# Two broadcast rows joined into one 4 KB-per-partition transfer, and a new due time for the added-up tiles

## The chip, the cores and the metric

The kernel runs on one core of one Trainium2 chip. The metric is the device time of one execution in microseconds (us), as the median of several runs. On the core, TensorE (PE), VectorE (DVE), ScalarE (ACT) and GpSimd (POOL) each follow their own instruction list in order; SyncE (SP) issues most of the DMAs, and POOL issues those that add one tile to another.

## The reference

Four graph layers are applied to `x` of shape (64, 256, 128): 64 graphs of 256 nodes with 128 features, all with one 256x256 matrix `adj`. Each layer is `x = x + layer(relu(layernorm(x)))`. Layer 0 is a gated recurrent unit of five steps, layer 1 a Chebyshev convolution, layer 2 a normalised convolution, layer 3 attention with an additive score. Nearly all the work lies in the score of layer 3:

```python
pre = s1[:, :, None, :] + s2[:, None, :, :] + b_lin      # (4 dims: graph, i, j, e)
h = jnp.where(pre >= 0, pre, ALPHA * pre)
e = jnp.einsum('bije,e->bij', h, a) + bias               # 256 features e
attn = jax.nn.softmax(e, axis=2)
out = jax.nn.sigmoid(jnp.einsum('bij,bjf->bif', attn, x))
```

For every graph and every pair of nodes (i, j) a piecewise linear function of 256 features is summed.

## The kernel before

**Units of work.** Two graphs form a pair, so there are 32 pairs (`NPAIR`). For each pair, `front(p)` computes layers 0 to 2 and the projections that the scores need. The scores themselves are cut into 64 slots a pair (`SLOTS`), and a slot covers four nodes i. For each slot two tiles `rl` of 128 x 2048 f32 (1 MB) are made, one from each half of the 256 features. DVE makes one tile of the first half in one instruction (L853), ACT makes one tile of the second half in eight (L867), and POOL makes tiles of either half in eight (L875). PE sums a tile over the features with four matmuls into a bank of 128 x 512 (L935, in `score`). `tail(p, ic)` turns a finished block of 32 slots into attention and output; there are two blocks a pair.

**Joined slots.** In 3 of 10 slots (`SHARE`, `WITH`) the two tiles are not both given to PE. `add_pair` (L890) lets a DMA, issued by POOL, add tile `z` onto tile `t` (L892), and PE then scores `t` once. There are 13 `rl` tiles in all, so `z` is wanted again for the next slots.

**The planner.** The order of the instructions on each engine is worked out when the program is built. A loop keeps a clock for each engine (`ran`) and for the SP queue (`moved`), and gives the next step to the engine whose clock stands lowest. Nothing of these clocks is left in the program but the order. A tile carries the planned time from which it may be used: `tile_ready` compares it, and `work_on_tile` takes the free tile with the earliest one. For an added-up tile, `add_pair` plans this time from `ISSUE`, `ADDED` and `LANDED` (L28): in `adding` the additions stand in a row of 5.2 us each, and 2.4 us are put on top. Both the freed `z` and the summed `t` get this time. If a planned time is too early, the engine that takes the tile stands still in the program until the DMA has landed, with all that stands behind it on that engine.

**The two rows.** The odd one of the 256 features is not scored on the tiles. Its contribution needs, for a pair, two rows of 512 numbers on all 128 partitions: `s2o` and `lin`. `front` makes both as a piece `quarter` of 128 partitions x 128 numbers, in which the numbers of the two rows stand on partitions 0, 32, 64, 96 and 1, 33, 65, 97. `quarter` is written to a DRAM tile `row` (L698). Two DMAs then read from it, `s2o` and `lin`, each with four pieces of 512 B a partition that stand 16 KB apart in `row` (L701); the source is the same for all partitions. `tail` uses `s2o` on DVE (L738) and `lin` on POOL (L748).

Of the kernel before, what the change touches and what calls it, by code (L numbers as in the profile page):

```python
# [8 lines left out]
F32 = mybir.dt.float32  # L9
# [5 lines left out]
P = 128  # L15
NB = 2
# [8 lines left out]
SHARE = (3, 10)  # L25
AHEAD_OF = 2
LOW = 1
ISSUE, ADDED, LANDED, SLACK = 0.65, 5.2, 2.4, 0.3  # L28


@with_exitstack
def kernel(
# [50 lines left out]
    nc = tc.nc  # L83
    B, N, D = x.shape
# [6 lines left out]
    work = ctx.enter_context(tc.tile_pool(name="work", bufs=2))  # L91
    relu_pool = ctx.enter_context(tc.tile_pool(name="relu", bufs=3))
    psum = ctx.enter_context(tc.tile_pool(name="psum", bufs=1, space=PSUM))
    dram = ctx.enter_context(tc.tile_pool(name="dram", bufs=4, space=bass.MemoryType.DRAM))
# [11 lines left out]
    def ran(engine, us, *after):  # L106
        start = max(clock[engine], 0.0, *after)
        if engine == ACT:
            behind[0] = max(0.0, behind[0] - (start - clock[ACT])) + 0.024 * us
        clock[engine] = start + us  # L110
        return clock[engine] + SEEN[engine] + (behind[0] if engine == ACT else 0.0)

    def moved(since):

        queue[0] = max(queue[0], since) + 0.5
        return queue[0] + 2.2
# [3 lines left out]
    def take():  # L120

        spare.sort(key=lambda b: b[1])
        return spare.pop(0)
# [7 lines left out]
    last, done = {}, [0]  # L131
# [268 lines left out]
    def flat(t):  # L400
        return t.rearrange("p b n -> p (b n)")
# [34 lines left out]
    def feat(name, **kw):  # L436
        return work.tile([P, NB, N], F32, name=name, **kw)
# [13 lines left out]
    def norm(src, since, h):  # L451

        stats = work.tile([P, NB * NC, 3], F32, name="stats")
        mv = work.tile([P, NB * NC, 2], F32, name="mv")
        s, h = rows_of(src), rows_of(h)[:, :, 0:D]
        yield DVE, since
        for k in range(0, NB * NC, 2):
            nc.vector.bn_stats(stats[:, k:k + 2, :].rearrange("p k s -> p (k s)"), s[:, k:k + 2, :].rearrange("p k d -> p d k"))
        t = ran(DVE, 0.8, since)
        yield POOL, t  # L460
        inverse_root(mv[:, :, 1], stats[:, :, 2], 1.0 / D, OP.mult, LN_EPS, OP.add)
        t = ran(POOL, 1.45, t)
        yield DVE, t
        nc.vector.scalar_tensor_tensor(mv[:, :, 0], stats[:, :, 1], -1.0, mv[:, :, 1], op0=OP.mult, op1=OP.mult)  # L464
        t = ran(DVE, 0.1, t)
        yield ACT, t
        for k in range(NB * NC):
            nc.scalar.activation(h[:, k, :], s[:, k, :], AF.Relu, bias=mv[:, k, 0:1], scale=mv[:, k, 1:2])  # L468
        return ran(ACT, 1.55, t)

    def copied(name, bank, t):

        c = feat(name, **(SHORT if name not in KEPT else KEPT[name]))
        nc.scalar.copy(c, by_feature(bank[0]))  # L474
        t = ran(ACT, COPY, t)
        spare.append([bank[0], t])
        return c, t
# [5 lines left out]
    def front(p):  # L483
# [8 lines left out]
        t = yield from norm(x0, 20.0 if p else 3.0, h)  # L492
        yield PE, t, 1
        b = take()
        to_feature(b[0], h)
        t_h = t
        t = ran(PE, TURN, t, b[1])
        yield ACT, t
        hT, t_hT = copied("hT", b, t)
        for step in range(STEPS):  # L500
            yield PE, t_h, 1, lambda: "adj" in SET_UP
            b = take()
            mix_nodes(b[0], h, adj_t)
            t = ran(PE, MIX, t_h, b[1])
            yield ACT, t
            mT, t_m = copied("mT", b, t)
            if p == 0:
# [6 lines left out]
                t = ran(PE, PROJECT, t_m)  # L514
# [3 lines left out]
            else:  # L518
# [4 lines left out]
                t = ran(PE, 2 * PROJECT, t_m, t_hT, pr[1])  # L523
# [3 lines left out]
            t = ran(ACT, TANH, t, r[1])  # L527
# [4 lines left out]
            if p == 0:  # L532
# [5 lines left out]
                t = ran(PE, PROJECT, t_rh)  # L538
            else:
# [7 lines left out]
                t = ran(PE, 2 * PROJECT, t_rh, pv[1])  # L547
# [6 lines left out]
            if p < 1:  # L554
                nc.scalar.activation(pv[0], pv[0], AF.Tanh, bias=bh, scale=1.0)
                t = ran(ACT, TANH, t)
                yield DVE, t
                nc.vector.tensor_sub(d, by_feature(pv[0]), hT)
                t = ran(DVE, ELEMENTS, t)
            else:  # L560
                nc.scalar.activation(d, by_feature(pv[0]), AF.Tanh, bias=bh, scale=1.0)  # L561
                t = ran(ACT, TANH, t)
# [3 lines left out]
                t = ran(POOL, 1.3, t)  # L566
            yield DVE, max(t, t_z)
            nc.vector.scalar_tensor_tensor(by_feature(pr[0]), by_feature(pr[0]), 1.0, d, op0=OP.add, op1=OP.mult)  # L568
            t = ran(DVE, ELEMENTS, t, t_z)
# [8 lines left out]
            b = take()  # L578
            to_token(b[0], hT)
            t = ran(PE, TURN, t_hT, b[1])  # L580
# [9 lines left out]
        t = ran(DVE, ELEMENTS, t)  # L590
# [6 lines left out]
        b = take()  # L597
        mix_nodes(b[0], h, adj_n)
        t = ran(PE, MIX, t_h, b[1])
# [3 lines left out]
        b = take()  # L603
        to_feature(b[0], h)
        t = ran(PE, TURN, t_h, b[1])
        yield ACT, t
        hT, t = copied("hT", b, t)
        yield PE, t_h, 1
        b = take()
        mix_nodes(b[0], h, adj_2)  # L610
        t = ran(PE, MIX, t_h, b[1])
        yield ACT, t
        c2T, t = copied("c2T", b, t)
# [3 lines left out]
        t = ran(PE, PRODUCTS, t, po[1])  # L617
# [3 lines left out]
        t = ran(DVE, ELEMENTS, t)  # L621
# [3 lines left out]
        t = ran(DVE, ELEMENTS)  # L625
# [4 lines left out]
        t = yield from norm(x2, t, h)  # L630
        yield PE, t, 1
        b = take()
        mix_nodes(b[0], h, adj_ti)
        t = ran(PE, MIX, t, b[1])
        yield ACT, t
        yT, t = copied("yT", b, t)
# [3 lines left out]
        t = ran(PE, PRODUCT, t, po[1])  # L640
# [3 lines left out]
        t = ran(DVE, ELEMENTS, t)  # L644
# [3 lines left out]
        t = ran(ACT, COPY, t)  # L648
# [3 lines left out]
        t = ran(DVE, ELEMENTS, t)  # L652
        yield POOL, t
        inverse_root(rn, rn, MOST_POSITIVE, OP.min, NORM_EPS * NORM_EPS, OP.max)
        t = ran(POOL, 1.35, t)
# [6 lines left out]
        t = ran(DVE, 1.04, t)  # L662
# [5 lines left out]
        t = yield from norm(x3, t, h3)  # L668
        yield PE, t, 1
        b = take()  # L670
        to_feature(b[0], h3)
        t = ran(PE, TURN, t, b[1])
# [11 lines left out]
        b = take()  # L684
# [4 lines left out]
        t = ran(PE, 0.6, t_hT, b[1])  # L689
        yield ACT, t  # L690
        quarter = work.tile([P, P], F32, name="quarter", bufs=1)
# [2 lines left out]
        nc.scalar.activation(s1o, b[0][:, P:P + NB * NC], AF.Identity, bias=b_odd, scale=1.0)  # L694
        t = ran(ACT, 0.35, t)
        spare.append([b[0], t])
        row = dram.tile([P, P], F32, name="row", bufs=2)
        nc.sync.dma_start(row, quarter)  # L698
        lin, s2o = feat("lin"), feat("s2o")
        for k, o in enumerate((s2o, lin)):  # L700
            nc.sync.dma_start(flat(o).rearrange("p (q n) -> p q n", q=4), row[1 - k:P:32, :].unsqueeze(0).to_broadcast([P, 4, P]))  # L701
            t = moved(t)
        t = moved(t)
        t_lin = t
        yield PE, t_hT, 1
        b = take()
        project(b[0], w2n[:, P:2 * P], hT)
        t = ran(PE, PROJECT, t_hT, b[1])
# [3 lines left out]
        b = take()  # L712
        project(b[0], w1[:, P:2 * P], hT)
        t = ran(PE, PROJECT, t_hT, b[1])
# [6 lines left out]
        b = take()  # L721
        project(b[0], w1[:, 0:P], hT)
        t = ran(PE, PROJECT, t_hT, b[1])
# [6 lines left out]
                        lin=lin, t_lin=t_lin, since=(max(t_n, t_s2a), max(t_b, t_2), max(t_b, t_2)))  # L730
# [77 lines left out]
    adding = [0.0]  # L808
# [81 lines left out]
    def add_pair(n):  # L890
        (since, t, e), (since_z, z, e_z) = pairs[n][0], pairs.pop(n)[2]
        nc.gpsimd.dma_start(out=t.rearrange("p g b n -> p (g b n)"), in_=z.rearrange("p g b n -> p (g b n)"), accum_op=OP.add)  # L892
        issued = ran(POOL, ISSUE, since, since_z)
        adding[0] = max(adding[0], issued) + ADDED
        done = adding[0] + LANDED
        held[e] -= 1
        held[e_z] -= 1
        tiles.append([z, done])
        made.append((done, n, 2, t, None))
# [53 lines left out]
    def begin_front():  # L953
        p = begun_fronts[0]
        if p > 0:
            load_x(p + 1)
        begin(p, front(p))
        begun_fronts[0] += 1
# [27 lines left out]
    while scored[0] < 2 * NSLOT or CHAINS:  # L986
# [20 lines left out]
        if ready:  # L1007
            if e == PE and len(tiles) <= LOW:
                ready = [x for x in ready if x[1] == (2,)] or ready
            _, (rank, *_), what = min(ready, key=lambda x: x[1])  # L1010
            if rank < 2:
                advance(what)
            elif e == PE:
                score(what)
            elif rank == 2:
                add_pair(what)
            else:
                work_on_tile(e)
            in_order()
            now[e] = max(now[e], clock[e])  # L1020
        else:
            later = [x[0] for x in todo] + [t for t in now.values() if t > now[e]]
            now[e] = min(later) if later else now[e] + 1.0
# [31 lines left out]
```

## Time and profile before

| What | Value |
|---|---|
| Median of 3 runs | 5011.35 us (5008.55 to 5022.84) |
| Profiled execution, its own time | 4997.03 us |
| Its span from the first to the last instruction | 4995.2 us |
| TensorE clock granted, mean | 0.993 of full speed |
| Busy: PE, DVE, ACT, POOL | 4851.9, 4659.2, 4664.4, 4662.2 us |
| DMA: adding DMAs (L892) | 614 of 1 MB each |
| DMA: `row`, `s2o`, `lin` | 32 each, of 64, 256 and 256 KB |
| Share of the 16 DMA engines' span taken by the POOL queue | 64.2% |

The busy times are those of the whole execution, with about 130 us at the start in which only the first pair's front runs. A DMA line of the profile gives the count, the size of each transfer, and the median time from its issue to its landing. An idle time is put down to what ended it.

### The profile page before, as it was taken

How to read it: one execution, taken by the hardware profiler on the slowest of the kernel's cores; microseconds unless marked ns; L12 is line 12 of the kernel's file. 1: busy time of each engine (PE TensorE's matmuls, PEld its weight loads, DVE VectorE, ACT ScalarE, POOL GpSimd, SP SyncE). 2: the span in 40 equal slices, each digit the busy share in tenths (PEclk: the TensorE clock that was granted, in tenths of full speed). 3: DMA queues.
4: the chain of work that ended last, by engine and by line, in shares of the span. 5: the costliest groups of instructions: out<-in, count | busy, mean ns of one | idle time of the engine just before them, and what ended most of it. 6: DMA issues, size and time to landing. Idle time of an engine off the chain costs nothing.

```text
span 4995.2 us, 134047 instructions
## 1 busy us (share of the span) xinstructions
PE 4851.9 (97%) x52487; PEld 1789.2 (36%) x52487; DVE 4659.2 (93%) x3289; ACT 4664.4 (93%) x12177; POOL 4662.2 (93%) x9446
## 2 busy tenths in 40 slices
PE   8999999999999999999999999999999999999988
PEld 3333333333333333333333333333333333333332
DVE  3999999999999999999999999999999999999998
ACT  3999999999999999999999999999999999999998
POOL 1999999999999999999999999999999999999997
PEclk9999999999999999999999999999999999999999
DMA  0667766677677676776676677776667766666677
GB/s 18 122 141 145 148 141 137 138 144 145 139 143 144 135 147 136 142 144 141 136 152 129 139 145 144 143 144 140 135 138 145 144 136 139 142 138 140 140 156 147
DMA packets 165644, 689.42 MB, mean 138 GB/s; under 512 B 14864, under 2 KB 86416, under 8 KB 86416
## 3 DMA queue, kind: packets, MB, share of 16 engines
q0 software_dynamic: 88416, 643.86, 64.2%
q1 hardware_dynamic: 75872, 36.98, 3.1%
q8 instruction: 410, 6.72, 0.5%
q14 instruction: 226, 1.85, 0.1%
q10 hardware_dynamic: 720, 0.00, 0.0%
HBM read 26.48 MB, written 10.49 MB: 7 GB/s over the span
## 4 chain that ended last, share of the span: by engine, by line
PE 55%; POOL 13%; DVE 13%; DMA 7%; ACT 7%; issue 4%; POOLq 0%; ACTq 0%; DVEq 0%
PE bank L935 32%; PE bank L398 19%; DVE rl L853 11%; POOL rl L875 10%; DMA rl<-rl 7%; ACT rl L867 5%; PE bank L426 2%; POOL rl L892 1%; PE bank L419 1%; POOL d L565 1%; DVE hT L572 1%; DVE bank L568 1%; PE bank L688 1%; PE bank L686 1%; ACT h L468 0%
## 5 line engine op out<-in xcount | busy, mean ns | idle before, releaser
L853 DVE TENSOR_TENSOR rl<-s1a,bank 128x2048 f32<-128x2048 f32 x1814 | 4060.1, 2277 | 173.7 <-PE bank L935 79.7
L867 ACT ACTIVATE rl<-bank,s1b 128x256 f32<-128x256 f32 x10128 | 4045.9, 757 | 144.8 <-PE bank L935 94.6
L875 POOL TENSOR_SCALAR rl<-s2n,s1b 128x256 f32<-128x256 f32 x6256 | 2949.0, 659 | 113.2 <-DMA rl<-rl 59.9
L935 PE MATMUL bank<-rl,win_n 128*32 128x512 f32 x17728 | 2227.4, 596 | 57.4 <-DVE rl L853 34.7
L935 PE MATMUL bank<-rl,win 128*32 128x512 f32 x10128 | 1335.5, 595 | 0.0
L935 PEld LDWEIGHTS bank<-rl,win_n 128*32 128x32 f32 x17728 | 559.0, 110 | 1235.2 <-issue 991.9
L875 POOL TENSOR_SCALAR rl<-s2c,s1a 128x256 f32<-128x256 f32 x1872 | 895.6, 655 | 14.3 <-DMA rl<-rl 7.0
L892 POOL DMA_DIRECT2D rl<-rl x614 | 567.8, 935 | 38.2 <-DVE rl L853 14.2
L935 PEld LDWEIGHTS bank<-rl,win 128*32 128x32 f32 x10128 | 327.3, 110 | 657.5 <-issue 534.5
L398 PE MATMUL bank<-mT,wts 128*32 128x512 f32 x2560 | 336.6, 592 | 1.3 <-DVE rh L530 1.3
L398 PE MATMUL bank<-adj_t,h 128*32 128x256 f32 x5120 | 308.7, 382 | 4.7 <-ACT h L584 4.7
L565 POOL TENSOR_TENSOR d<-d,hT 128x512 f32<-128x512 f32 x155 | 219.4, 1416 | 66.6 <-ACT d L561 66.6
L398 PEld LDWEIGHTS bank<-adj_t,h 128*32 128x32 f32 x5120 | 164.8, 111 | 179.9 <-issue 62.1
L468 ACT ACTIVATE h<-x,mv 128x128 f32<-128x128 f32 x384 | 187.8, 806 | 6.1 <-DVE mv L464 6.0
L398 PE MATMUL bank<-rh,u5t 128*32 128x512 f32 x1280 | 172.4, 601 | 15.3 <-DVE rh L530 15.3
L398 PE MATMUL bank<-mT,w 128*32 128x512 f32 x1280 | 170.6, 594 | 0.0
L398 PE MATMUL bank<-hT,wts 128*32 128x512 f32 x1280 | 167.8, 593 | 0.0
L561 ACT ACTIVATE d<-bank,gate_b 128x512 f32<-128x512 f32 x155 | 145.3, 937 | 22.6 <-PE bank L398 22.4
L526 ACT ACTIVATE bank<-bank,gate_b 128x512 f32<-128x512 f32 x160 | 138.3, 864 | 20.4 <-PE bank L398 19.5
L398 PEld LDWEIGHTS bank<-mT,wts 128*32 128x32 f32 x2560 | 83.6, 110 | 193.8 <-issue 152.1
L549 ACT ACTIVATE bank<-bank,gate_b 128x512 f32<-128x512 f32 x160 | 146.7, 917 | 6.7 <-PE bank L398 6.7
L474 ACT COPY mT<-bank 128x512 f32<-128x512 f32 x160 | 127.5, 797 | 26.1 <-PE bank L398 25.8
(166 smaller groups left out, 3501.2 us busy)
## 6 DMA issues: line engine op xcount, KB each, us to landing
rl<-rl POOLq DMA_DIRECT2D x614, 1024.0 KB, 8.0
xin<-in_x_dram SPq DMA_DIRECT2D x64, 128.0 KB, 4.7
s2o<-row SPq DMA_DIRECT2D x32, 256.0 KB, 8.6
lin<-row SPq DMA_DIRECT2D x32, 256.0 KB, 11.0
out_dram<-o SPq DMA_DIRECT2D x64, 128.0 KB, 4.6
row<-quarter SPq DMA_DIRECT2D x32, 64.0 KB, 2.9
w_raw<-in_L_gnn_w_w_dram SPq DMA_DIRECT2D x3, 128.0 KB, 2.6
th_raw<-in_L_gnn_Theta_dram SPq DMA_DIRECT2D x1, 320.0 KB, 3.5
```

Of the source, the lines that this page charges most:

```text
L398: nc.tensor.matmul(o[g:g + 32], w[:, g:g + 32], t, start=start, stop=stop, skip_group_check=True)
L468: nc.scalar.activation(h[:, k, :], s[:, k, :], AF.Relu, bias=mv[:, k, 0:1], scale=mv[:, k, 1:2])
L474: nc.scalar.copy(c, by_feature(bank[0]))
L526: nc.scalar.activation(r[0], pr[0], AF.Tanh, bias=br, scale=0.5)
L549: nc.scalar.activation(pr[0], pr[0], AF.Tanh, bias=bz, scale=0.5)
L561: nc.scalar.activation(d, by_feature(pv[0]), AF.Tanh, bias=bh, scale=1.0)
L565: nc.gpsimd.tensor_sub(d, d, hT)
L853: nc.vector.tensor_tensor(t, rows.to_broadcast(whole), ops["s2a"].unsqueeze(1).to_broadcast(whole), op=OP.min)
L867: nc.scalar.activation(t[:, g, b, :], s2p[:, b, :], AF.Relu, bias=ops["s1"][1][:, b, i:i + 1], scale=-1.0)
L875: nc.gpsimd.tensor_scalar(t[:, part, b, :], ops["s2n" if k else "s2c"][:, b, :], ops["s1"][min(k, 1)][:, b, row], MOST_NEGATIVE, op0=OP.mi ...
L892: nc.gpsimd.dma_start(out=t.rearrange("p g b n -> p (g b n)"), in_=z.rearrange("p g b n -> p (g b n)"), accum_op=OP.add)
L935: nc.tensor.matmul(pe[g * 32:(g + 1) * 32, :], w[:, 31 - r:63 - r], flat(t[:, g]), start=False, stop=(left[block] == 0), skip_group_check= ...
```

## The change

The change has two parts. In `front`, the DRAM tile `row` becomes 2 x 512 numbers, each of the two rows contiguous, and one after the other. Two DMAs of four partitions each write it. One DMA then reads the whole 4 KB for each of the 128 partitions into one SBUF tile `rows`, of which `lin` and `s2o` are the two halves. The planned time of arrival (`t_lin`) is changed with it. In `add_pair`, the planned time of a summed tile is worked out in another way: 6.6 us after its issue, or 5.3 us after the addition before it, whichever is later.

```diff
-ISSUE, ADDED, LANDED, SLACK = 0.65, 5.2, 2.4, 0.3
+ISSUE, ADDED, LANDED, SLACK = 0.65, 5.3, 6.6, 0.3
...
-        row = dram.tile([P, P], F32, name="row", bufs=2)
-        nc.sync.dma_start(row, quarter)
-        lin, s2o = feat("lin"), feat("s2o")
-        for k, o in enumerate((s2o, lin)):
-            nc.sync.dma_start(flat(o).rearrange("p (q n) -> p q n", q=4), row[1 - k:P:32, :].unsqueeze(0).to_broadcast([P, 4, P]))
-            t = moved(t)
-        t = moved(t)
+        row = dram.tile([2, NB * N], F32, name="row", bufs=2)
+        for k in range(2):
+            nc.sync.dma_start(row[k].rearrange("(q n) -> q n", q=4), quarter[k:P:32, :])
+            t = moved(t) if k else max(t, moved(t) - 2.2)
+        rows = work.tile([P, 2, NB, N], F32, name="rows")
+        nc.sync.dma_start(rows.rearrange("p k b n -> p (k b n)"), row.rearrange("k t -> (k t)").unsqueeze(0).to_broadcast([P, 2 * NB * N]))
+        lin, s2o = rows[:, 0], rows[:, 1]
+        t = moved(t) + 1.5
         t_lin = t
...
         issued = ran(POOL, ISSUE, since, since_z)
-        adding[0] = max(adding[0], issued) + ADDED
-        done = adding[0] + LANDED
+        done = adding[0] = max(adding[0] + ADDED, issued + LANDED)
```

## The prediction

> **What bounds the kernel now.** I read the busy times first, then the waits, then the DMA issues, then one stretch in time.
>
> ```profile
> PE 4851.9 (97%) x52487; PEld 1789.2 (36%) x52487; DVE 4659.2 (93%) x3289; ACT 4664.4 (93%) x12177; POOL 4662.2 (93%) x9446
> ...
> DVE rl L853 <- PE bank L935: 79.7, 108, 2.9
> DVE rl L853 <- DMA rl<-rl: 76.8, 28, 7.9
> POOL rl L875 <- DMA rl<-rl: 66.9, 18, 7.8
> ACT rl L867 <- DMA rl<-rl: 46.0, 21, 6.2
> PE bank L935 <- DMA rl<-rl: 21.6, 20, 4.9
> ...
> rl<-rl POOLq DMA_DIRECT2D x614, 1024.0 KB, 8.0
> s2o<-row SPq DMA_DIRECT2D x32, 256.0 KB, 8.6
> lin<-row SPq DMA_DIRECT2D x32, 256.0 KB, 11.0
> row<-quarter SPq DMA_DIRECT2D x32, 64.0 KB, 2.9
> ```
>
> All four engines are close to full, so no idle time is free. The waits for the adding DMA (us, times, longest) are few but long: up to 7.9 us. Where they lie shows in the timeline around one broadcast, from answers for SP, POOL and DVE, with the landing times of that stretch and of a quiet one before it, and with three windows (the last two numbers are the DMA share and GB/s):
>
> ```profile
> 2060.70 0.36 SPq L701 DMA_DIRECT2D s2o<-row  x1
> 2061.11 0.50 SPq L701 DMA_DIRECT2D lin<-row  x1
> 2060.86 1.04 POOL L892 DMA_DIRECT2D rl<-rl  x1
> 2077.39 8.88 DVE L853 TENSOR_TENSOR rl<-s1a,bank 128x2048 f32<-128x2048 f32 x4 [6.35 <-DMA rl<-rl]
> 2082.65 3.61 POOL L875 TENSOR_SCALAR rl<-s2n,s1b 128x256 f32<-128x256 f32 x8 [6.87 <-DMA rl<-rl]
> ...
> DMA to landing us min/median/max: 15.8/16.2/16.5
> DMA to landing us min/median/max: 7.3/7.5/7.6
> ...
> 127.50:139.00 11.50, 8.15 (x77) 2.19 (x69) 9.13 (x9) 10.51 (x28) 9.66 (x21) 0.98 0.23 47
> 2062.00:2067.00 5.00, 5.00 (x72) 2.24 (x68) 3.55 (x5) 4.47 (x14) 4.83 (x11) 1.00 0.24 39
> 2072.00:2078.00 6.00, 5.40 (x56) 1.56 (x52) 0.61 (x1) 6.00 (x16) 3.78 (x9) 1.00 1.04 216
> ```
>
> The addition issued at 2060.86 lands after 16.5 us, where 7.5 is usual, and the two behind it are as late. While the broadcasts flow, the DMA engines move 39 GB/s at a share of 0.24; when the addition moves, 216. The first pair's broadcast (127.5 to 139) has no addition beside it and still gets 47 GB/s. So the two broadcasts are slow in themselves (512 KB at 45 GB/s is 11.4 us), and an addition stands behind them with idle DMA engines.
>
> I then laid a window from 10 to 35 us after the s2o issue on each of pairs 1 to 31, and one from 40 to 65 us. Their sums, in this order:
>
> ```profile
> sum 775.00, PE 720.85 PEld 223.09 DVE 656.53 ACT 682.94 POOL 674.77; mean PE 23.25 PEld 7.20 DVE 21.18 ACT 22.03 POOL 21.77
> sum 775.00, PE 757.53 PEld 251.32 DVE 763.24 ACT 768.67 POOL 760.27; mean PE 24.44 PEld 8.11 DVE 24.62 ACT 24.80 POOL 24.52
> ```
>
> After a broadcast, DVE, ACT and POOL lose 107, 86 and 85 us more than in the quiet windows (763.24 - 656.53, and so on), 93 on average; PE loses 37 more. Over 130 to 4960 us the windows view gives PE 4723.88 us busy of 4830, which leaves 106 idle.
>
> **What the Trainium skill says.** "DMA: Bandwidth & Descriptors" has three places. Its section "Issuing engines are not separate DMA queues" says that DMAs of SP and POOL share the same 16 engines and interleave; the trace agrees that they share, at 16.5 against 7.5 us. Its section "Queues, rings and completion order" says that an engine alternates between queues packet by packet; the trace does not look like that, as the addition waits for most of s2o. Its section "Latency and other measured facts" reports copies from HBM rows at large power-of-two pitches running at half rate, and suspects channels that are hit in lockstep. No trace here has such rows, but the 47 GB/s from pieces 16 KB apart, the same for every partition, could be of that kind. The section "Anatomy of one DMA" gives 2.0 us + bytes/436e3: an estimate of 3.2 us for 512 KB. For the 1 MB addition it gives 4.4, where the trace's shortest is 6.7, so I use it as a lower end only.
>
> **The change part by part.**
>
> 1. *Three transfers of a pair.* Before, SP issues `row`, `s2o`, `lin`: 0.34 + 0.36 + 0.95 us. After, two writes and one read, about the same; SP mostly waits for other engines (1743.7 us for `x` alone), so this costs nothing, and out_dram stores behind it have no reader on the chip. The writes use four partitions each, which no row shows: between the shortest `row` landing (1.5 us) and the longest (9.8); I take 3.
> 2. *The broadcast.* Both move 512 KB. Pieces fall from 1024 of 512 B to 128 of 4 KB. If the pace goes by pieces or by the 16 KB pitch, the flow falls from 11.4 us to between 1.2 (512 KB at 436 GB/s) and 3 us (four times the pace of now); if it goes by bytes from one place, it stays at 11.4. I take 3. Nobody waits for `rows` itself: the first L738 after the load at 2060.70 runs at 2126.35, 65 us later.
> 3. *The additions.* Of the 614, 86 overlap a broadcast or queue behind one that does; they land after 12.3 us on average, the others after 8.1 (both from the trace's records). The excess 4.2 falls with the flow, by some 3/4.
> 4. *What this is worth.* If the three elementwise engines alone set the pace, all of 93 us comes back; if PE does, only its 37. Both limits bind in turn: DVE also waits 79.7 us for PE to free tiles, and the 106 us of PE idle include waits that stay (31.9 for hT of L572, 16.5 for rh of L530). For a full cure I take 60, between 37 and 93; three quarters of it is 45.
> 5. *The due times.* A lone addition is planned to land 0.65 + 0.13 + 5.2 + 2.4 = 8.4 us after its start before (0.13 is the planner's POOL constant), 0.65 + 0.13 + 6.6 = 7.4 after. In a row the step is 5.3 instead of 5.2. The trace has 7.3 (median of the lone ones) and 5.3. So the plan becomes right at the median and loses 1 us of margin. In the trace I followed each tile of the 528 additions outside the broadcasts to its next user: the next writer of `z` starts a median 3.0 us after the landing, but 112 start within 1.2 us; for PE on `t` 56 start within 1.5 us. Were every one of these due 1.1 us sooner, the writers would wait 67 us more in all, 22 per engine, and PE 31. The program is also re-sorted: the PE list differs in most places, though the counts hold (1813 L853 instead of 1814, 235 groups of eight L875 `s2c` instead of 234). Tiles free 1 us sooner may give some of it back. I take a loss of 5, between a gain of 15 and a loss of 31. Behind a waiting L853 stand the hT and rh steps on DVE, for which PE waits.
>
> Sum against the profiled execution: 4997 - 45 + 5 = 4957 us. The median of the runs stands 14 above that execution, so the forecast is 4971.
>
> **Rivals.**
>
> *The flow stays slow, and the plan does no harm.* The change then doesn't do what it says for the additions. For it: 47 GB/s with no addition in flight may be the pace of reading one place, whatever the piece. Against it: 16 KB between pieces is a special address step, and the change takes it away. Gain 0, plan -5 to +10: 5005 to 5020.
>
> *Slower: the margin in the due times is missed.* Place: the next writer of `z` (L853, L867, L875) and L935 on `t`. Price: 22 to 31 us as in part 5, and more if late landings stay, since the plan then expects tiles in 7.4 us that come in 12 to 16. It decides from the point at which the stall brings back less than about 10 us. Time: 5011 + 30 = 5041. For it are the 112 writers within 1.2 us; against it the usual slack of 3.0 us for writers and 5.0 for PE.
>
> *The elementwise engines set the pace throughout.* The whole 93 us and a better plan: 5011 - 93 - 5 = 4913. Against it: PE would be left with some 10 us of idle time in 4800.
>
> **How the numbers follow.** A measurement of this kernel can tell about 0.3% (15 us) from no change. I give the forecast's case (a gain of 16 to 75 us) 0.64, the full return 0.04, the slow flow without harm 0.16 and the missed margin 0.16. Faster is 0.68, same 0.16, slower 0.16. The range goes from 4920, near the full return, to 5020, the top of the slow flow; the missed margin is left out.
>
> **What would show it.** Right: `rows<-row` lands within about 5 us, additions next to it within 9 to 10, their longest is well below 18.3, and the waits on `DMA rl<-rl` of DVE, POOL and ACT, 190 us together now, fall below 100. Part 5 is wrong if these waits stay small per wait but grow in number away from the broadcasts. The forecast is wrong if `rows<-row` takes over 10 us, or if PE is as idle as before (106 us) while the long waits are gone.

## The result, and the profile after

The changed kernel takes 4958.24 us (median of 4 runs, 4956.34 to 4965.92) against 5013.7 for the kernel before (median of 4): a ratio of 0.989, with a 95% interval of 0.9872 to 0.9909. The profiled execution of after is 4965.92 us, of before 4997.03. The latter lies 17 us below the median of its kernel, so the two traces show only 31 of the 55 us.

The page of the kernel after, with busy times and DMA issues (no landing is recorded for `rows`, as for other SP transfers of this run):

```profile
PE 4840.3 (98%) x52487; PEld 1793.6 (36%) x52487; DVE 4663.4 (94%) x3288; ACT 4672.1 (94%) x12177; POOL 4684.9 (94%) x9454
...
rl<-rl POOLq DMA_DIRECT2D x614, 1024.0 KB, 7.9
rows<-row SPq DMA_DIRECT2D x32, 512.0 KB
```

The waits of the kernel after for the adding DMA (us in total, times, longest):

```profile
DVE rl L854 <- DMA rl<-rl: 39.1, 32, 3.7
ACT rl L868 <- DMA rl<-rl: 36.6, 24, 3.4
PE bank L935 <- DMA rl<-rl: 25.8, 27, 3.2
POOL rl L876 <- DMA rl<-rl: 16.6, 19, 2.0
```

DVE, ACT and POOL together wait 92 us instead of 190. But the number of their waits has not fallen: 75 now, 67 before. The long ones are gone (3.7 at most, 7.9 before), and short ones have come.

The same pair as before in the timeline of the kernel after, with the landing times of the additions issued from 2055 to 2085 us, and the window in which the broadcast flows:

```profile
2059.22 0.34 SPq L702 DMA_DIRECT2D rows<-row  x1
2061.58 0.75 POOL L893 DMA_DIRECT2D rl<-rl  x1
...
DMA to landing us min/median/max: 7.2/7.4/9.0
...
2060.00:2063.00 3.00, 3.00 (x40) 1.10 (x36) 3.00 (x2) 3.00 (x8) 3.00 (x7) 1.00 0.72 210
```

While the broadcast flows the DMAs move 210 GB/s instead of 39, and no engine but PE's weight loads is idle in that window. By the trace's records the last of the 128 pieces ends a median 5.7 us after the issue (3.2 to 9.4). The additions in flight together with a broadcast land after 8.9 us on average; in the kernel before it was about 12.

The windows from 10 to 35 us after each `rows` issue, and from 40 to 65, for pairs 1 to 31 of the kernel after:

```profile
sum 775.00, PE 770.38 PEld 245.77 DVE 741.52 ACT 742.43 POOL 753.64; mean PE 24.85 PEld 7.93 DVE 23.92 ACT 23.95 POOL 24.31
sum 775.00, PE 758.62 PEld 258.34 DVE 756.42 ACT 768.29 POOL 759.38; mean PE 24.47 PEld 8.33 DVE 24.40 ACT 24.78 POOL 24.50
```

After a broadcast the three elementwise engines now lose 15, 26 and 6 us more than in the quiet windows, where it was 107, 86 and 85. PE loses nothing there.

### The profile page after: what moved, and what is told of

Same layout as the page of the kernel before. It is cut to its first block, busy times and chain, and to the rows that moved or that the text cites. A ratio compares the mean times of both kernels' runs of the same rounds, so it can differ in the third digit from the quotient of the medians.

```text
span 4964.1 us, 133991 instructions
## 1 busy us (share of the span) xinstructions
PE 4840.3 (98%) x52487; PEld 1793.6 (36%) x52487; DVE 4663.4 (94%) x3288; ACT 4672.1 (94%) x12177; POOL 4684.9 (94%) x9454
## 3 DMA queue, kind: packets, MB, share of 16 engines
q14 instruction: 225, 1.84, 0.1%
## 4 chain that ended last, share of the span: by engine, by line
PE 58%; POOL 11%; DVE 8%; DMA 4%; ACT 4%; issue 3%; POOLq 0%; DVEq 0%; ACTq 0%
PE bank L935 36%; PE bank L398 18%; POOL rl L876 8%; DVE rl L854 6%; DMA rl<-rl 4%; ACT rl L868 3%; PE bank L426 2%; POOL rl L893 1%; PE bank L688 1%; PE bank L686 1%; PE bank L419 1%; POOL d L565 1%; DVE mv L464 0%; POOL mv L393 0%; DVE hT L572 0%
## 5 line engine op out<-in xcount | busy, mean ns | idle before, releaser
L935 PE MATMUL bank<-rl,win_n 128*32 128x512 f32 x17728 | 2198.3, 595 | 56.6 <-DVE rl L854 29.7
```

The costliest lines, as they stand in the source:

```text
L935: nc.tensor.matmul(pe[g * 32:(g + 1) * 32, :], w[:, 31 - r:63 - r], flat(t[:, g]), start=False, stop=(left[block] == 0), skip_group_check= ...
```

## The experiments

**The two parts, each alone.** The planned arrival of the rows turned out not to change the order: with one part alone, every instruction of the four engines stands exactly where it stands in the kernel before (rows alone) or after (due times alone). So with these two runs and the changed kernel, each step is a change either of the broadcast or of the order. The changed kernel was run again as the mark.

> The changed kernel once more, as the mark for the other runs of this chip. Every theory expects a ratio of 0.989 to the kernel before, some 4958 us where that has 5013.

Measured: 4969.38 us against 5015.43 of before on this chip; ratio 0.9905 (0.9889 to 0.9922).

The joined rows with the old due times:

```diff
-ISSUE, ADDED, LANDED, SLACK = 0.65, 5.3, 6.6, 0.3
+ISSUE, ADDED, LANDED, SLACK = 0.65, 5.2, 2.4, 0.3
...
-        done = adding[0] = max(adding[0] + ADDED, issued + LANDED)
+        adding[0] = max(adding[0], issued) + ADDED
+        done = adding[0] + LANDED
```

> The joined broadcast alone, with the due times of before; PE, DVE, ACT and POOL have their instructions in exactly the order of before. Theory A (an addition stood behind the slow broadcast, and the new due times cost a little): 10 to 15 us faster than the changed kernel, a ratio of about 0.987 to before, and the waits for the adding DMA away from the broadcasts stay at some 35 us over DVE, ACT and POOL. Theory B (the due times bring the gain): hardly faster than before, a ratio over 0.996.

Measured: 4934.2 us, ratio 0.984 (0.9824 to 0.9856). That is 81 us below before and 35 below the changed kernel, more than theory A expected on both sides. Its waits for the adding DMA:

```profile
ACT rl L868 <- DMA rl<-rl: 20.0, 16, 2.5
POOL rl L876 <- DMA rl<-rl: 13.6, 9, 2.5
DVE rl L854 <- DMA rl<-rl: 9.0, 11, 1.8
PE bank L936 <- DMA rl<-rl: 8.4, 13, 2.3
```

43 us over the three engines, of which 33 lie away from the broadcasts (35 in the kernel before).

The new due times with the old broadcasts (the diff is the one above the other way round, on the kernel before):

> The new due times alone, with the two broadcasts of before; the four engines have exactly the order of the changed kernel. Theory A: 10 to 30 us slower than before (ratio 1.002 to 1.006), additions next to a broadcast land after 12 us or more, and the long waits for them are back. Theory B: a ratio of about 0.99 to before.

Measured: 5075.34 us, ratio 1.0124 (1.0107 to 1.0141), so 60 us slower than before. Both theories are off: the direction is A's, the size twice what A gave. Its waits:

```profile
DVE rl L853 <- DMA rl<-rl: 107.4, 52, 8.8
POOL rl L875 <- DMA rl<-rl: 76.8, 30, 7.7
ACT rl L867 <- DMA rl<-rl: 72.7, 28, 8.4
PE bank L934 <- DMA rl<-rl: 48.5, 38, 5.3
```

The long waits are back and the short ones have been added. The additions beside a broadcast land after about 12 us, as in the kernel before. So the rows bring 81 us, and the due times take back 35 beside the fast broadcast and 60 beside the slow one.

**The full cure.** The broadcasts of the kernel before are taken away altogether, except the first pair's. All pairs use that pair's rows, so this kernel leaves out the rows of the other 31:

```diff
...
-        lin, s2o = feat("lin"), feat("s2o")
+        if p == 0:
+            KEEP.update(lin=const.tile([P, NB, N], F32, name="lin"), s2o=const.tile([P, NB, N], F32, name="s2o"))
+        lin, s2o = KEEP["lin"], KEEP["s2o"]
         for k, o in enumerate((s2o, lin)):
+            if p == 0:
...
```

> The kernel before with its order, but the two broadcasts run for the first pair only, and all pairs use its rows: 31 pairs have no broadcast (the rows of the other pairs are left out of the scores). This is the full cure of the stall. Theory A: 60 us faster than before, between 37 and 93 (ratio 0.988, 0.981 to 0.993), and within 10 us of the joined broadcast with the order of before. Theory C (the joined broadcast still costs much): 20 us or more below the run with the joined broadcast.

Measured: 4930.2 us, ratio 0.9833 (0.9817 to 0.9848). Theory A holds in its upper part: by the medians the broadcasts of before cost 85 us (between the two profiled executions, 4997.03 and 4930.98, it is 66). The joined broadcast with the same order is 4 us above that, which the intervals do not tell from nothing. Theory C falls.

**What makes the broadcast slow.** Three things changed at once: the piece (512 B to 4 KB), the count of transfers, and the place in DRAM. Here the piece and the two transfers of before are kept, and only the step between the eight pieces of a pair is varied, all in the changed kernel's order (the comment lists the widths of the five runs):

```diff
-        row = dram.tile([2, NB * N], F32, name="row", bufs=2)
+        row = dram.tile([8, 128], F32, name="row", bufs=2)     # 128, 1024, 2048, 4096 or 4224
         for k in range(2):
-            nc.sync.dma_start(row[k].rearrange("(q n) -> q n", q=4), quarter[k:P:32, :])
+            nc.sync.dma_start(row[k:8:2, 0:P], quarter[k:P:32, :])
...
-        nc.sync.dma_start(rows.rearrange("p k b n -> p (k b n)"), row.rearrange("k t -> (k t)").unsqueeze(0).to_broadcast([P, 2 * NB * N]))
+        for k in range(2):
+            nc.sync.dma_start(flat(rows[:, k]).rearrange("p (q n) -> p q n", q=4), row[k:8:2, 0:P].unsqueeze(0).to_broadcast([P, 4, P]))
```

The pieces of one transfer are two steps apart, and the second transfer's lie one step further. So within one transfer the pieces stand 1, 8, 16, 32 or 33 KB apart; in the kernel before it is 16 KB.

> As the changed kernel, with all four engines in its order, but the rows are read in two transfers of four pieces of 512 B per partition again. The eight pieces stand side by side in 4 KB of DRAM. Theory P (the pace goes by the number of pieces): the flow of 512 KB takes some 11 us as before, and the time is near that of the new due times alone, 5075 us. Theory S (the step of 16 KB between pieces is what slows it) and theory N (what counts is how wide a stretch of addresses is read): a flow of 3 to 5 us and a time near 4969.

> As the run before it, but the eight pieces of 512 B stand 16 KB apart in DRAM. Theories P and S: a flow of 11 us or more, about 5075 us. Theory N (a wide stretch of addresses helps): 3 to 5 us, near 4969.

> As the run before it, but the eight pieces of 512 B stand 16.5 KB apart. Theory P: a flow of 11 us, about 5075 us. Theory S: the flow falls to 3 to 5 us and the time to about 4969. Theory N: the same as S.

> As the run with eight pieces of 512 B 16 KB apart, but 8 KB apart. If only steps of 16 KB and their multiples meet in one place, the flow is as fast as with the pieces side by side (5 us to landing for each half) and the time about 4955; if 8 KB is enough, 8 to 12 us to landing and over 5020.

> The same with the pieces 4 KB apart: fast (5 us to landing, about 4955) unless a step of 4 KB is enough to meet in one place (8 to 12 us, over 5020).

The DMA issues of these five runs, in the order of the table below (count, KB, median us to landing of one half, over the 14 transfers of each run whose landing is recorded):

```profile
rows<-row SPq DMA_DIRECT2D x64, 256.0 KB, 5.2
...
rows<-row SPq DMA_DIRECT2D x64, 256.0 KB, 5.1
...
rows<-row SPq DMA_DIRECT2D x64, 256.0 KB, 9.1
...
rows<-row SPq DMA_DIRECT2D x64, 256.0 KB, 13.8
...
rows<-row SPq DMA_DIRECT2D x64, 256.0 KB, 11.8
```

| Step between the eight pieces | Apart within one transfer | Time, us | Ratio to before (95%) |
|---|---|---|---|
| 512 B (side by side) | 1 KB | 4951.23 | 0.9887 (0.9872 to 0.9902) |
| 16.5 KB | 33 KB | 4953.04 | 0.989 (0.9875 to 0.9905) |
| 4 KB | 8 KB | 5026.86 | 1.0018 (1.0011 to 1.0025) |
| 8 KB | 16 KB | 5152.99 | 1.0268 (1.025 to 1.0285) |
| 16 KB | 32 KB | 5103.31 | 1.0193 (1.0176 to 1.021) |
| changed kernel, one transfer of 4 KB pieces | one piece | 4969.38 | 0.9905 (0.9889 to 0.9922) |

These runs come from three chips, so it is the ratios that compare; the one with 8 KB was executed twice only.

Theory P falls: the same 1024 pieces of 512 B land in 5.2 us when they stand side by side, and the time is the changed kernel's within the intervals. Theory N falls as well, as a wide stretch in steps of 16 KB is the slow one. S holds: adding 512 B to the step of 16 KB cures it. Steps of 4 and 8 KB are slow too, but they do not tell how small a step can be and still be slow. In the run with 8 KB the pieces of each transfer stand 16 KB apart, as in the kernel before, so it does not test the first of the two answers that it was to choose from, that only multiples of 16 KB meet in one place. In the run with 4 KB they stand 8 KB apart, and one half lands in 9.1 us, between the fast runs and the other two. Whether 8 KB is a bad distance in itself, or every second of these pieces still meets at 16 KB, is not separated. Why steps of 8 and 16 KB cost more than the broadcasts of before in the same order (5153 and 5103 against 5075 us) also stays open. For the change the answer is clear: neither the 4 KB piece nor the single transfer was needed for the gain, as the run with the pieces side by side has neither. What was needed is that the pieces of one transfer no longer stand 16 KB apart.

**The due times, one number at a time.** All with the joined rows. Here the planned landing of a lone addition, `LANDED`, is moved from 6.6 to 7.6, 8.6 and 5.6, and the step stays at 5.3. At 7.6, only the step differs from the due times of before (5.2 + 2.4 is 7.6).

> The changed kernel with 7.6 in place of 6.6 for a lone addition, which is what the due times of before give (5.2 + 2.4); the step of 5.3 stays. Theory M (the margin of 1 us in the due time of a lone addition is what the new plan lost): within 10 us of the joined broadcast with the due times of before, 4934 us. Theory T (the longer step of 5.3 us, or any change of order, costs it): near the changed kernel, 4969 us.

> The changed kernel with 8.6 in place of 6.6 for a lone addition, 1 us more than the due times of before. Theory M (margin): no slower than with 7.6, a ratio of 0.980 to 0.986 to before, and still fewer waits for the adding DMA. Theory R (a tile that comes back later in the plan is missed by the engines): 10 us or more slower than with 7.6, ratio over 0.988.

> The changed kernel with 5.6 in place of 6.6: a lone addition is planned to land 1 us before the median of the trace. Theory M: another 30 us or more slower than the changed kernel, about 5000 us and a ratio over 0.995, with more waits for the adding DMA. Theory O (each order has its own luck of 20 to 30 us and the margin is not the cause): anywhere between 4930 and 5000 us.

| LANDED, ADDED | Time, us | Ratio to before (95%) | Waits of DVE, ACT, POOL for the adding DMA in the profiled execution, us |
|---|---|---|---|
| 5.6, 5.3 | 5045.71 | 1.0051 (1.0034 to 1.0068) | 160 |
| 6.6, 5.3 (changed kernel) | 4969.38 | 0.9905 (0.9889 to 0.9922) | 95 |
| 7.6, 5.3 | 4936.34 | 0.9858 (0.9843 to 0.9873) | 33 |
| 7.6, 5.2 (due times of before) | 4934.2 | 0.984 (0.9824 to 0.9856) | 43 |
| 8.6, 5.3 | 4925.44 | 0.9819 (0.9807 to 0.9832) | 11 |

The waits views of the two ends, first 5.6, then 8.6:

```profile
DVE rl L854 <- DMA rl<-rl: 67.2, 57, 4.4
ACT rl L868 <- DMA rl<-rl: 52.7, 41, 3.8
POOL rl L876 <- DMA rl<-rl: 40.5, 36, 4.0
```

```profile
DVE rl L854 <- DMA rl<-rl: 5.8, 6, 1.8
ACT rl L868 <- DMA rl<-rl: 4.7, 3, 2.7
POOL rl L876 <- DMA rl<-rl: 0.9, 2, 0.5
```

These runs too come from three chips. The profiled execution with 5.6 took 5024.04 us, 22 below its median, so its 160 us of waits go with that time. From 5.6 to 8.6, time and waits fall together, so theory M holds against T, O and R. The longer step is not to blame: 5.3 and 5.2 give the same within the intervals. An order's own luck of 20 to 30 us could be mixed into single steps, but it would hardly put all four values of `LANDED` in line, and 5046 lies above the range that theory O gave. Theory R does not begin to show at 8.6. With 8.6 the kernel beats both: 4925.44 us, ratio 0.9819, some 43 us below the changed kernel by the difference of the ratios (0.9905 - 0.9819, of 5015).

## Why the prediction was right, and where it was wrong

The forecast was 4971 us, and the kernel takes 4958. The direction, the place and the mechanism of the gain held. That the number came so close is luck. Two terms of the sum were mis-sized, and their errors nearly cancelled: by the medians the rows brought 81 us where 45 were forecast, and the due times took 35 where 5 were. The third term, the 14 us by which the runs were to lie above the profiled execution, did not carry over: the profiled execution of the changed kernel lies 8 us above its median.

- *The stall (what bounds the kernel, and parts 2 and 3).* Right. The additions stood behind the broadcast; with the flow at 210 GB/s they land in 8.9 us and the excess idle after a broadcast is nearly gone. The cause of the slow flow was left open between pieces and step. It is the step.
- *What it is worth (part 4).* Too low. "For a full cure I take 60" measured 85 by the medians, and the three quarters became nearly all, 81. Part of the gap lies in the yardstick: the 37 and the 93 were read from one execution that took 4997.03 us, 18 below the median on the chip of these runs. From that execution to those of the runs without broadcasts and with the rows alone it is 66 and 65 us. So the 60 was near for the execution that it was worked out from, and the three quarters was the larger error there. The rival in which the elementwise engines set the pace throughout has 93 for this term, near the 85 but not near the 66; these runs do not decide between it and the two limits in turn. PE's 37 was too low in any case: with the rows alone PE is busy for 4840.8 us of 4930.4, which is 90 us idle instead of 143, and it is 11 us less busy. The busy time was not fixed; the section on the hardware below shows what moves it.
- *The due times (part 5).* Wrong in size. "I take a loss of 5, between a gain of 15 and a loss of 31" measured 35. The prediction's own test shows the place: these waits were to grow in number away from the broadcasts, and in the profiled executions those of DVE, ACT and POOL went from 23 to 55 there, from 35 to 71 us. The waits themselves were not taken too low. From the rows alone to the changed kernel (4969.38 us) they rose by 52 us over the three engines and by 16 on PE, below the 67 and 31 worked out; away from the broadcasts, where these were worked out, by 40 and 14. The error was to treat 22 per engine and PE's 31 as two ends of a range, and to expect the re-sorting to give something back. A mean of 17 per engine and 16 on PE come to 33 when they are added, near the 35. That they add is argued from the sizes, not shown. From 6.6 to 5.6 the same sum gives 46, where the profiled executions differ by 54.
- *The slower rival.* Its mechanism was at work all along; it was only outweighed. Its price of 22 to 31 us was too low, as above, and with the slow broadcast left in it is 60. So its point of decision was too low as well: beside a loss of 35, a cure that brought less than that would have left the kernel slower.
- *The slow flow.* Did not come. It could have: with pieces in steps of 4 KB the flow stayed slow in part, and the time was 5027 us.
- *Parts 1 and 2, on the arrival of the rows.* Right to cost it at nothing: the order does not change with it. The broadcast was put at 3 us; the pieces of the pair shown flow for 2.4 us and end 3.4 after the issue, but over all pairs the last ends a median 5.7 after it.

## What to carry to other kernels

A change of two parts can be right in sum with one part wrong: run each part alone before keeping both. A due time in a fixed order is no estimate but a promise for an engine that can do nothing else meanwhile; set it above the median of what it plans for, and try a few values. Here the best of the four stands for a landing about 9.4 us after the start of the issue (0.65 + 0.13 + 8.6), where the median of a lone addition is 7.3; whether a still later one is better was not tried. Watch the step between pieces in DRAM that all partitions read: in steps of 4, 8 or 16 KB a half of these rows landed in 9 to 14 us, and side by side, or with 512 B added to the step of 16 KB, in 5.

## What the runs showed of the hardware

**Starving PE also costs it clock.** The granted clock of these runs goes down with the stalls; the work is the same 52487 matmuls. The cores view of the rows alone, of the kernel before, and of the run with steps of 8 KB, in which PE is idle for 90, 143 and 253 us:

```profile
core 0: 4930.4 us, clock 0.995
...
core 0: 4995.2 us, clock 0.993
...
core 0: 5151.1 us, clock 0.984
```

In the clock records PE runs at half speed for 49, 70 and 169 us in these three, 22, 50 and 128 of it after the first 200 us. The stretches are 3.41 us or a multiple of it, but for the last one of each run, and after the first 200 us they all start on one grid of 3.41 us. Laid out in windows along this grid, without the last 40 us and the windows that were at half speed already, the kernel before has ten windows that are followed by half speed. Each of them holds 1.86 to 3.16 us of PE idle time, and no other window holds more than 1.84. Over all 14 traces it is 123 windows of at least 1.78 us against 19209 others, of which two reach 2.0. So in these traces PE fell to half speed when it had been idle for somewhat more than half of one window of 3.41 us; the bound is rough, as the profile's ends of matmuls are modelled. The Trainium skill's "TensorE: Matmul & The Clock Gate", section "Part 1: The HAM clock gate", tells of half clock after an idle window of about 3.4 us. The length of the window agrees, but here the window need not be idle throughout.

The price on PE can be estimated: with the rows alone it is at half speed for 21 us less than in the kernel before, which is worth half of that, 10.5 us, and its busy time fell by 11. No run took the stalls away and kept the half clock, so how much of a kernel's loss is this one stays open.

**A slow read holds back the other queue's DMA.** An addition issued beside a broadcast that moved at 39 GB/s had to wait for it, though the DMA engines were busy for a quarter of the time. The first 8 KB packet of the one at 2060.86 us starts 7.1 us after the issue, where it is 1.3 to 1.5 for the four lone additions ahead of it. Beside the same bytes and the same 1024 pieces from neighbouring addresses it did not: the additions beside that one landed after some 8.6 us on average. Whether the pieces meet in one part of the DRAM or in the address handling of the DMA was not tried.
